# Moving the two kinds of transposes of an attention into the first gap of each step

## The chip, the cores and the metric

The kernel runs on one core of a Trainium2 chip. The metric is the time of one execution on the device in microseconds. The profile shows five engines: TensorE (PE; its weight loads are listed apart as PEld), VectorE (DVE), ScalarE (ACT), GpSimd (POOL) and SyncE (SP), which here only issues transfers. All data is 32-bit floating point.

## The reference

Eight batch items of 1024 tokens with 256 features pass through two layers. Each layer normalizes its input and adds the outputs of an attention and of a feed-forward part to it:

```python
xn = layernorm(x)
x = x + causal_attention(xn) + top1_experts(xn)      # 16 heads of 16, 8 experts, softmax router
xn = layernorm(x)
x = x + metric_attention(xn) + butterfly_ffn(xn)     # 16 heads of 16, 256 -> 1024 -> 256
```

In the first attention a query may see the keys up to itself (masked scores are a large negative number and not left out, so a small term for the masked keys stays in numerator and denominator). The second attention has no mask; its queries are multiplied by a metric computed from the input. In both, with one head's queries, keys and values:

```python
prob = softmax(q @ k.T / 4)
out  = prob @ v
```

The change concerns this attention. The experts and the butterfly part matter only as other work that TensorE does in between.

## The kernel before

**Units.** There are 16 attentions: the causal one (tiles named `_a`) and the unmasked one (`_b`) of each of the eight items, in an order that interleaves the two layers of neighbouring items. An attention has four groups `g` of four heads, and a group has two halves `h` of 512 queries. A half runs over tiles of 128 keys, `kt`: eight in the unmasked attention, four or eight in the causal one. One such (`g`, `h`, `kt`) is a *step*. A step has two parts `pr`, each for two of the group's four heads. I call the room for other work after the scores of part 0 the *first gap* and after those of part 1 the *second gap*.

**Scores and their maxima.** `exp_step` (its matmuls are L478) computes transposed scores of two heads, each with 32 rows of the array, into a pair of PSUM banks `sc`; ScalarE takes the exponential into `p` (L485), and in the causal attention GpSimd sets masked elements to zero (L487). The maximum of each query has to be known by then. So a first pass runs ahead: `max_step` computes scores with queries on the partitions into a pair of banks `mx` (L435), and VectorE reduces them to `mm` (L444). In the loop, `first_pass(1 - pr ...)` follows `exp_step(pr)`, so that the two use different rows of the array and run at once.

**Turn of the maxima.** When a half's maxima are complete, `maxima` writes their negatives to `negmax`, queries on the partitions. `put_max` (L464) turns them into the layout of Q^T with four 128x128 transposes into a pair bank `nm` (L468), and VectorE adds them to Q^T in a row that was kept free (L470). The local function `put(until)` (L1333) calls it for halves that became ready before half-step `until`; at the beginning of a half whatever is needed is put in any case.

**Weighing, and turn of the weighed values.** `weigh` (L500, matmuls L503) multiplies the exponentials with the values of four heads, each head 32 columns of the array, and sums over `kt` in the bank `av`. It runs one step late: in the first gap of a step it takes the `pair` of the step before, kept in `held`. When it has taken the last `kt` of a half, ScalarE copies `av` to `u` (L514), and the inner function returns what `norm` needs, which is kept in `turned`. `norm` (L517) turns `u` with four transposes into a pair bank `ut` (L523). In the unmasked attention VectorE then takes the reciprocal of the denominators (L550) and multiplies (L551). In the causal one GpSimd first prepares the terms for masked keys, `es` (L537) and `ec` (L542), and VectorE adds them (L546, L548) before the same two operations. The result goes to `on`, which the output projection reads later through `outputs`.

**Order and buffers.** The program order is written by hand. Pair banks come from a ring of three (`ps_sc`), used in turn by `sc`, `mx`, `nm`, `ut` and some of the other work; `av` has one bank, and other work has one (`ps_ms`). The projections of the next group of heads (`project0`, `project1`: tiles `q`, `k`) are called in both gaps of some steps as `urgent`; all else (experts, butterflies, normalization, output projections) is given out by `Fill`, which spends estimated costs against due times, mostly in the second gap. Neither kind of turn has a cost in these estimates, so where turns stand does not influence what `Fill` gives out.

## Time and profile before

| | |
|---|---|
| median of three runs | 4849.75 us (4848.44 to 4857.87) |
| the profiled execution's own time | 4851.03 us |
| its span, first to last instruction | 4849.3 us |
| mean granted TensorE clock | 0.988 |
| TensorE busy | 4665.7 us |
| VectorE, ScalarE, GpSimd busy | 3090.5, 2215.8, 765.0 us |
| scores and maxima's scores, `sc_b`, `mx_b` (L478, L435) | 1141.2, 1154.2 us, overlapping |
| weighing, `av_b`, `av_a` (L503) | 554.1, 338.9 us |
| turn of weighed values, `ut_a`, `ut_b` (L523) | 42.2, 41.8 us, 64 of four transposes each |
| turn of maxima, `nm_a`, `nm_b` (L468) | 44.9, 42.0 us, 64 of four transposes each |

Columns of a time line are start and duration in us, engine, line, operation, output<-inputs, shape and count; a bracket at the end gives how long the engine had been idle and what released it. In this profile a matmul of two 32-bit operands has two records and a transpose one, so a turn is x4 and the weighing of one part's two heads x4 as well; the time line merges neighbours. Busy times of one group are unions in time; groups that run in different rows of the array overlap.

### The profile page before, as it was taken

Reading aid. Unit: us, or ns where it says so; the run is one execution under the profiler, and the core shown is the slowest. Engines: PE = TensorE matmul, PEld = TensorE weight load, DVE = VectorE, ACT = ScalarE, POOL = GpSimd, SP = SyncE. Lnnn points to the kernel's source line nnn. Section 1 sums busy time; section 2 is a strip of 40 time slices with the busy share of each in tenths; the row PEclk is TensorE's granted clock in tenths of the full one; section 3 lists DMA queues with packets and bytes.
Section 4 is the critical chain, followed back from the end, with each engine's and each line's share of the span. In section 5 each row is a group of like instructions: output and inputs, shape, how many; then the busy total and the mean of one; then the engine's idle time right before and its main releaser. Section 6 shows DMA issues by size and latency. Waiting matters only on the chain.

```text
span 4849.3 us, 69199 instructions
## 1 busy us (share of the span) xinstructions
PE 4665.7 (96%) x27808; PEld 1865.1 (38%) x27808; DVE 3090.5 (64%) x5048; ACT 2215.8 (46%) x2925; POOL 765.0 (16%) x1340
## 2 busy tenths in 40 slices
PE   6899999999999999999999999999999999999998
PEld 3343344344333443334433444334443344433332
DVE  6776665665766567665676656766567665666553
ACT  2443444543454344543445434454345543454544
POOL 4232202111021110211112021111111111110000
PEclk8999999999999999999999999999999999999999
DMA  4122101120001200011000110001100110000000
GB/s 162 59 67 66 34 1 32 34 74 14 1 18 39 73 15 1 24 41 67 14 2 29 51 52 13 7 28 53 46 12 9 32 53 32 20 1 10 1 10 9
DMA packets 85680, 158.28 MB, mean 33 GB/s; under 512 B 12656, under 2 KB 67568, under 8 KB 82160
## 3 DMA queue, kind: packets, MB, share of 16 engines
q1 hardware_dynamic: 69616, 89.88, 5.5%
q0 software_dynamic: 15744, 63.98, 4.3%
q8 instruction: 220, 3.60, 0.3%
q14 instruction: 100, 0.82, 0.1%
HBM read 117.25 MB, written 36.57 MB: 32 GB/s over the span
## 4 chain that ended last, share of the span: by engine, by line
PE 88%; DVE 7%; ACT 3%; DMA 1%; issue 1%; POOL 0%; POOLq 0%; DVEq 0%; SPq 0%; ACTq 0%
PE sc_b L478 18%; PE av_b L503 10%; PE sc_a L478 10%; PE mx_b L435 6%; PE av_a L503 6%; PE w L1164 5%; PE mx_a L435 5%; PE f L390 5%; PE g_b L1091 3%; PE h_b L390 2%; PE e L811 2%; DVE mm_a L444 2%; ACT p_b L485 1%; PE q_a L390 1%; PE k_a L390 1%; PE q_b L390 1%
## 5 line engine op out<-in xcount | busy, mean ns | idle before, releaser
L444 DVE TENSOR_REDUCE mm_b<-mx_b 128x2 f32<-128x1024 f32 x1024 | 1251.5, 1223 | 756.6 <-PE mx_b L435 755.8
L485 ACT ACTIVATE p_b<-sc_b 128x1024 f32<-128x1024 f32 x1024 | 1044.8, 1023 | 1105.3 <-PE mx_b L435 619.1
L435 PE MATMUL mx_b<-kT_b,qT_b 32*128 32x512 f32 x4096 | 1154.2, 640 | 10.6 <-ACT p_b L485 6.8
L478 PE MATMUL sc_b<-qT_b,kT_b 32*128 32x512 f32 x4096 | 1141.2, 638 | 8.7 <-ACT p_b L485 2.6
L485 ACT ACTIVATE p_a<-sc_a 128x1024 f32<-128x1024 f32 (+3 forms) x768 | 620.1, 809 | 916.8 <-PE sc_a L478 640.4
L444 DVE TENSOR_REDUCE mm_a<-mx_a 128x2 f32<-128x1024 f32 (+3 forms) x768 | 733.9, 957 | 218.3 <-PE mx_a L435 199.2
L478 PE MATMUL sc_a<-qT_a,kT_a 32*128 32x512 f32 (+3 forms) x3072 | 713.3, 542 | 9.0 <-DVE mm_a L444 6.9
L435 PE MATMUL mx_a<-kT_a,qT_a 32*128 32x512 f32 (+3 forms) x3072 | 707.2, 542 | 10.2 <-ACT p_a L485 4.9
L503 PE MATMUL av_b<-p_b,vals 128*32 128x512 f32 x4096 | 554.1, 605 | 1.5 <-ACT p_b L485 1.5
L478 PEld LDWEIGHTS sc_b<-qT_b,kT_b 32*128 32x128 f32 x4096 | 305.9, 183 | 625.9 <-issue 418.3
L440 DVE TENSOR_TENSOR mx_a<-mx_a,cst 128x256 f32<-128x256 f32 x512 | 219.8, 429 | 342.0 <-PE mx_a L435 153.3
L487 POOL TENSOR_SCALAR_AFFINE_SELECT p_a<-p_a 128x256 f32<-128x256 f32 x512 | 210.0, 412 | 1410.0 <-ACT p_a L485 1380.1
L478 PEld LDWEIGHTS sc_a<-qT_a,kT_a 32*128 32x128 f32 x3072 | 235.6, 186 | 384.2 <-issue 269.8
L503 PE MATMUL av_a<-p_a,vals 128*32 128x512 f32 (+3 forms) x3072 | 338.9, 505 | 0.8 <-POOL spacer_a L707 0.7
L435 PEld LDWEIGHTS mx_b<-kT_b,qT_b 32*128 32x128 f32 x4096 | 306.3, 183 | 54.5 <-ACT p_b L485 39.9
L1164 PE MATMUL w<-wcon,f 128*128 128x256 f32 x1024 | 273.7, 396 | 0.0
L796 POOL DMA_INDIRECT ew<-in_ew,rows_a x120 | 116.5, 971 | 959.3 <-PE mx_b L435 443.0
L435 PEld LDWEIGHTS mx_a<-kT_a,qT_a 32*128 32x128 f32 x3072 | 233.9, 186 | 57.5 <-ACT p_a L485 33.9
L503 PEld LDWEIGHTS av_b<-p_b,vals 128*32 128x32 f32 x4096 | 81.7, 108 | 392.2 <-issue 383.2
L1164 PEld LDWEIGHTS w<-wcon,f 128*128 128x128 f32 x1024 | 178.2, 189 | 139.3 <-issue 114.5
L390 PE MATMUL f<-xT_b,wexp 128*128 128x512 f32 x512 | 223.9, 595 | 0.0
L503 PEld LDWEIGHTS av_a<-p_a,vals 128*32 128x32 f32 x3072 | 62.6, 108 | 265.4 <-issue 207.2
(215 smaller groups left out, 4232.4 us busy)
## 6 DMA issues: line engine op xcount, KB each, us to landing
ew<-sorted_d SPq DMA_DIRECT2D x120, 128.0 KB, 3.1
mixed_d<-ew SPq DMA_DIRECT2D x120, 128.0 KB, 1.7
x<-in_x SPq DMA_DIRECT2D x8, 1024.0 KB, 5.5
wexp<-wexp_d SPq DMA_DIRECT2D x8, 1024.0 KB, 7.6
wcon<-wcon_d SPq DMA_DIRECT2D x8, 1024.0 KB, 4.9
out<-x SPq DMA_DIRECT2D x8, 1024.0 KB, 5.0
paths<-in_paths SPq DMA_DIRECT2D x7, 1024.0 KB, 13.4
w<-in_w1t SPq DMA_DIRECT2D x8, 512.0 KB, 3.9
```

Source lines behind the costliest of these rows:

```text
L390: PE.matmul(ps, w[:, c, cols : cols + P], rhs[:, c, h * 512 : (h + 1) * 512], start=(c == 0), stop=(c == 1),)
L435: PE.matmul(sc[:, j, :w], qT[r : r + 32, t * P : (t + 1) * P], kT[r : r + 32, k * 512 : k * 512 + w], start=True, stop=True,)
L440: DVE.tensor_tensor(sc[:, :, w - P : w], sc[:, :, w - P : w], negmask.unsqueeze(1).to_broadcast([P, 2, P]), ALU.add,)
L444: DVE.tensor_reduce(mm[:, t, 2 * pr : 2 * pr + 2, k], sc[:, :, :w], AX.X, ALU.max)
L478: PE.matmul(sc[:, j, c0:], kT[r : r + 32, kt * P : (kt + 1) * P], qT[r : r + 32, h * 512 + c0 : (h + 1) * 512], start=True, stop=True,)
L485: ACT.activation(p[:, :, c0:], sc[:, :, c0:], AF.Exp, scale=0.25)
L487: POOL.affine_select(p[:, :, c0 : c0 + P], p[:, :, c0 : c0 + P], [[0, 2], [1, P]], ALU.is_ge, 0.0, base=0, channel_multiplier=-1,)
L503: PE.matmul(av[32 * i : 32 * i + 32, c0:], self.vals[:, kt, 4 * (g // 2) + i, odd : odd + 2, :].rearrange("p e d -> p (e d)"), p2[i // 2][ ...
L796: POOL.indirect_dma_start(halves[:, s % 2, : 3 * D], None, a["ew"], bass.IndirectOffsetOnAxis(ap=rows[:, s : s + 1], axis=0),)
L811: PE.matmul(ps[:, :D], was[:, c * P : (c + 1) * P], w[:, c * D : (c + 1) * D], start=(c == 0), stop=(c == 1),)
L1091: PE.matmul(ps, w2t[:, m, c * P : (c + 1) * P], hT[:, m, :], start=(m == 0), stop=(m == 3),)
L1164: PE.matmul(ps[:, :D], hT[k // 4][:, k % 4, i * P : (i + 1) * P], wcon[:, k, :], start=(k == 0), stop=(k == 7),)
```

## The change

In the first gap, the loop now calls `norm` for a finished half if one waits in `turned`, then the weighing of `held`, then `put`. In the second gap it calls none of the three. Before, the first gap had the weighing and then `put`; the second gap had `norm` and then `put`. A half that finishes its weighing in the first gap of a step was turned in the second gap of the same step; it is now turned in the first gap of the next step. The calls after the loop and the mandatory `put` at the start of a half are as they were.

```diff
                     for j in range(quota()):
                         first_pass(1 - pr if j == 0 else pr)
-                    if pr == 0 and held is not None:
-                        turned = weigh(*held)
-                    elif turned is not None:
-                        turned[0].norm(*turned[1:])
-                        turned = None
-                    put(now - 1)
+                    if pr == 0:
+                        if turned is not None:
+                            turned[0].norm(*turned[1:])
+                            turned = None
+                        if held is not None:
+                            turned = weigh(*held)
+                        put(now - 1)
                     if urgent is not None:
```

## The prediction

> **What bounds the kernel now.** I read the page first (busy time, then the chain that ended last), then the groups of instructions by shape, and then the time line of TensorE alone around two places where the moved work stands now. From the page: TensorE is busy for 96% of the span, and 88% of the chain lies on it; VectorE is busy for 64% and ScalarE for 46%. So the question is what each move does to the sequence on TensorE, and which short waits lie in it.

> ```profile
> PE 4665.7 (96%) x27808; PEld 1865.1 (38%) x27808; DVE 3090.5 (64%) x5048; ACT 2215.8 (46%) x2925; POOL 765.0 (16%) x1340
> ...
> PE 88%; DVE 7%; ACT 3%; DMA 1%; issue 1%; POOL 0%; POOLq 0%; DVEq 0%; SPq 0%; ACTq 0%
> ```

> The time line of TensorE shows three steps in the second attention, at 3054.18, 3059.14 and 3063.79. Columns: start, duration, engine, line, operation, tiles. I read starts, not durations, because the ends are modelled. `av` is the weighing, `nm` the turn of the maxima, `ut` the turn of the weighed values, `y` a piece of other work, `sc` and `mx` the scores (second rounds left out).

> ```profile
> 3054.18 1.06 PE L503 MATMUL av_b<-p_b,vals 128*32 128x512 f32 x8
> 3055.18 0.66 PE L468 MATMUL nm_b<-cst,negmax 128*128 128x128 f32 x4
> 3055.77 0.70 PE L478 MATMUL sc_b<-qT_b,kT_b 32*128 32x512 f32 x2
> ...
> 3056.84 1.13 PE L867 MATMUL y_a<-outw,oT_a 128*128 128x256 f32 x4
> 3057.90 0.70 PE L478 MATMUL sc_b<-qT_b,kT_b 32*128 32x512 f32 x2
> 3058.08 0.70 PE L435 MATMUL mx_b<-kT_b,qT_b 32*128 32x512 f32 x2
> ...
> 3059.14 1.06 PE L503 MATMUL av_b<-p_b,vals 128*32 128x512 f32 x8
> 3060.13 0.70 PE L478 MATMUL sc_b<-qT_b,kT_b 32*128 32x512 f32 x2
> ...
> 3061.27 0.66 PE L523 MATMUL ut_b<-cst,u_b 128*128 128x128 f32 x4
> 3061.76 1.03 PE L867 MATMUL y_a<-outw,oT_a 128*128 128x256 f32 x4
> 3062.72 0.70 PE L478 MATMUL sc_b<-qT_b,kT_b 32*128 32x512 f32 x2
> ...
> 3063.79 1.06 PE L503 MATMUL av_b<-p_b,vals 128*32 128x512 f32 x8
> 3064.78 0.70 PE L478 MATMUL sc_b<-qT_b,kT_b 32*128 32x512 f32 x2
> 3065.03 0.70 PE L435 MATMUL mx_b<-kT_b,qT_b 32*128 32x512 f32 x2
> ...
> 3066.09 1.13 PE L867 MATMUL y_a<-outw,oT_a 128*128 128x256 f32 x4
> ...
> 3068.22 0.64 PE L503 MATMUL av_b<-p_b,vals 128*32 128x512 f32 x4
> ```

> Four readings. A weighing alone takes 0.99 (3059.14 to 3060.13). A turn behind the weighing takes 0.59 more (3055.18 to 3055.77). A turn ahead of a piece of other work takes only 0.39 more: `ut` and `y` together 1.45 (3061.27 to 3062.72), `y` alone 1.06 (3056.84 to 3057.90). And there is a short wait: at 3064.78 `sc` starts and `mx` beside it only at 3065.03, so that this round of scores lasts 1.31 instead of 1.07. On ScalarE's time line the exponential of the scores before runs from 3063.95 to 3064.97; it holds the PSUM buffer that `mx` is to get. In the step with the turn of the maxima that wait (0.24) is filled, but 0.18 of it comes back after `y` (3057.90 to 3058.08). The steps last 4.96, 4.65 and 4.43.

> The second place is a step that computes the next projection, where `q` stands behind the weighing and `k` in the second gap:

> ```profile
> 3096.34 1.06 PE L503 MATMUL av_b<-p_b,vals 128*32 128x512 f32 x8
> ...
> 3100.32 0.66 PE L523 MATMUL ut_b<-cst,u_b 128*128 128x128 f32 x4
> 3100.82 1.98 PE L390 MATMUL k_b<-vT_b,wqk 128*128 128x512 f32 x4
> ...
> 3103.81 1.07 PE L503 MATMUL av_b<-p_b,vals 128*32 128x512 f32 x8
> ...
> 3108.29 1.98 PE L390 MATMUL k_b<-vT_b,wqk 128*128 128x512 f32 x4 [0.43 <-DVE qT_b L1116]
> ...
> 3111.27 0.64 PE L503 MATMUL av_b<-p_b,vals 128*32 128x512 f32 x4
> ```

> The step with the turn lasts 7.47, the one without 7.46: the turn sits in time in which `k` would wait for VectorE to empty the single small PSUM bank (0.43 in the second step). Here the turn is free today.

> **The change part by part.** I compared the instruction order of both kernels, engine by engine. Without the lines of `norm`, all five engines have the same order in both. So the turn of the maxima, `put_max`, moves nowhere: it stood in a first gap already (124 of its 128 directly behind a weighing). That part costs and gains nothing, and neither DMA nor ScalarE nor SyncE issues anything in another order. What moves is `norm`: 127 of its 128 turns go from the second gap of a step to the first gap of the next, ahead of the weighing. No instruction is added or removed.

> On TensorE, 118 of the 127 stood ahead of other work with the same 128x128 shape, 9 stood alone between scores. Going through the trace step by step, 31 turns are in a projection step followed by another one, 84 have an ordinary piece behind them and one in the next step, and 12 lack one of the two.

> The price in the new place is not in the trace: a weighing always follows scores there. Two rows are near: 0.59 for a turn and a weighing in one gap in the other order, 0.39 for a turn whose neighbour has its own shape. I take 0.59, because the neighbour is the weighing and its shape (128x32) differs from the turn's; 0.39 stays as the lower end. It cannot be below that where no wait is next to it, as TensorE does the same four products.

> [...]

> Projection steps: the second gap saves nothing (7.47 against 7.46, the wait for `q` takes the turn's place), the first gap has no wait to fill (scores behind `q` take 1.07). 31 x 0.59 = +18.3; lower end 31 x 0.39 = 12.1.

> Ordinary steps: the second gap saves 0.39. The first gap costs 0.59, fills the wait of 0.24, and 0.18 returns after the piece behind it; that is the step at 3054.18 against the one at 3063.79, 4.96 - 4.43 = 0.53. 0.53 - 0.39 = 0.14. Without the 0.18 (a long piece behind, which covers the exponential) it is -0.04; where the trace has no wait behind the weighing (28 of the 84) it is 0.20; with the saving read from whole steps (4.65 - 4.43 = 0.22) it is 0.31. I take 0.13, near the first and a little under it for the long pieces: 84 x 0.13 = +10.9, ends 84 x (-0.04) = -3 and 84 x 0.31 = +26.

> The other 12: alone between scores, where the exponential sets the pace, a turn is partly hidden today; between -0.4 (its 0.59 really saved, the wait filled at the new place) and +0.59. I take 0.1: +1.2.

> VectorE and GpSimd: per turn VectorE has 0.67 (0.25 + 0.42) in the second attention and 1.25 (0.41, 0.17, 0.25, 0.42) in the first; they move behind the reduction of the next scores (1.22). Nothing on TensorE needs the result before the output projection, several steps on. What waits is the PSUM buffer, reused one round later; the turn of the maxima, with 0.69 on VectorE in the same gap, shows scores at 1.07 behind it, so I cost this at 0. On GpSimd, `es` and `ec` (0.62 and 0.22) of 41 causal turns go behind masks (25, 0.41 each) and gathers (18, about 0.97): VectorE waits longer for `es`, now 17 us in 19 waits. It idles 0.9 before the next reduction, which hides most of that; if not, see the third rival.

> Sum: 18.3 + 10.9 + 1.2 = +30.4. The profiled execution took 4851.0 (span 4849.3 and 1.7 around it), 1.3 above the median of the runs. 4851.0 + 30.4 - 1.3 = 4880.

> **The rivals.** Against no change I count 0.2%, 9.7 us, about what a measurement of this kernel can tell.

> 1. No price for going from the turn to the weighing: each of the three groups falls by 0.20 a turn. 31 x 0.39 + 84 x (-0.07) + 12 x (-0.1) = 12.1 - 5.9 - 1.2 = +5: 4855, no measurable change. For it: turn to `y` is free. Against: weighing to turn is not.

> 2. Faster: VectorE is what holds the scores up. Today `norm`'s 0.67 or 1.25 stand right behind a reduction in the second gap; moved, all that VectorE gives back in that gap comes earlier. Over the affected pairs of steps, the rounds of scores next to the old and the new place last 39 us over 1.07 each, and the projections' waits come to 17.4: 56 in all. The gross price without any wait filled is 127 turns x 0.59 less 84 x 0.39, or 42; the change is faster once over 42 of the 56 vanish, and all 56 gone would make 4850 - 14 = 4836. Against: most of these waits end with ScalarE's exponential, and VectorE sat idle for 1.63 before it took `q`.

> 3. Slower than forecast: the 41 causal turns whose `es` queues behind GpSimd's masks and gathers hold VectorE, and with it the PSUM buffers. At 0.6 each, +25: 4905.

> **How the numbers follow.** Forecast 0.71, first rival 0.12, second 0.08, third 0.09. The predicted time is 4880. The range 4854 to 4900 takes in the first rival and the upper end of the sum (18.3 + 26 + 7 = 51, nearly), and leaves out the second and third. Slower 0.80 (forecast and third), same 0.12, faster 0.08.

> **What would show it.** In the profile after: `ut` starts, then `av` about 0.59 later (0.39 if the first rival holds); scores behind such a gap at 1.07, and `mx` 0.18 late after the next piece; projection steps with the turn near 8.05, those that lost it still near 7.46 with a wait for `qT`. I am wrong if `av` follows `ut` at 0.4, if the waits for VectorE in projection steps go away, or if scores behind the new place wait for `mm`.

## The result, and the profile after

| | before | after |
|---|---|---|
| median of four runs each | 4852.57 us (4848.44 to 4857.87) | 4884.23 us (4881.49 to 4888.69) |
| the profiled execution's own time | 4851.03 us | 4884.23 us |
| its span | 4849.3 us | 4882.5 us |
| mean granted TensorE clock in it | 0.988 | 0.985 |

The changed kernel takes 1.007 times as long (95% interval 1.0057 to 1.0082), 31.7 us more. The page of the changed kernel, busy time and chain:

```profile
PE 4687.2 (96%) x27808; PEld 1864.1 (38%) x27808; DVE 3099.1 (63%) x5048; ACT 2214.6 (45%) x2925; POOL 764.0 (16%) x1340
...
PE 87%; DVE 7%; ACT 3%; DMA 1%; issue 1%; POOL 1%; SPq 0%; POOLq 0%; DVEq 0%; ACTq 0%
```

The counts of instructions are the same as before, TensorE has 21.5 us more and is still busy for 96%. So nothing new bounds the kernel; its own sequence got longer. The time line of TensorE in the changed kernel, for the two steps that answer to those at 3059.14 and 3063.79 before (columns: start, duration, engine, line, operation, tiles):

```profile
3082.27 1.06 PE L503 MATMUL av_b<-p_b,vals 128*32 128x512 f32 x8
3083.27 0.70 PE L478 MATMUL sc_b<-qT_b,kT_b 32*128 32x512 f32 x2
...
3084.40 1.13 PE L867 MATMUL y_a<-outw,oT_a 128*128 128x256 f32 x4
3085.46 0.70 PE L478 MATMUL sc_b<-qT_b,kT_b 32*128 32x512 f32 x2
3085.58 0.70 PE L435 MATMUL mx_b<-kT_b,qT_b 32*128 32x512 f32 x2
...
3086.64 0.66 PE L523 MATMUL ut_b<-cst,u_b 128*128 128x128 f32 x4
3087.22 1.06 PE L503 MATMUL av_b<-p_b,vals 128*32 128x512 f32 x8
3088.22 0.70 PE L478 MATMUL sc_b<-qT_b,kT_b 32*128 32x512 f32 x2
3088.23 0.70 PE L435 MATMUL mx_b<-kT_b,qT_b 32*128 32x512 f32 x2
...
3089.29 1.13 PE L867 MATMUL y_a<-outw,oT_a 128*128 128x256 f32 x4
3090.35 0.70 PE L478 MATMUL sc_b<-qT_b,kT_b 32*128 32x512 f32 x2
3090.53 0.70 PE L435 MATMUL mx_b<-kT_b,qT_b 32*128 32x512 f32 x2
...
3091.59 0.64 PE L503 MATMUL av_b<-p_b,vals 128*32 128x512 f32 x4
```

From `ut` to `av` it is 0.58 (3086.64 to 3087.22). The scores behind the gap last 1.07 (3088.22 to 3089.29), and `mx` is 0.18 late behind the piece `y` (3090.35 to 3090.53). The step that lost the turn lasts 4.37 instead of 4.65: it saves 0.29 and not 0.39, because there too `mx` is now a little late behind `y` (0.12, 3085.46 to 3085.58). The step that got it lasts 4.95 instead of 4.43.

The second place, two steps with a projection, same view of the changed kernel:

```profile
3119.54 1.06 PE L503 MATMUL av_b<-p_b,vals 128*32 128x512 f32 x8
3120.53 1.98 PE L390 MATMUL q_b<-vT_b,wqk 128*128 128x512 f32 x4
...
3124.02 1.98 PE L390 MATMUL k_b<-vT_b,wqk 128*128 128x512 f32 x4 [0.43 <-DVE qT_b L1116]
...
3127.01 0.65 PE L523 MATMUL ut_b<-cst,u_b 128*128 128x128 f32 x4
3127.59 1.06 PE L503 MATMUL av_b<-p_b,vals 128*32 128x512 f32 x8
3128.59 1.98 PE L390 MATMUL q_b<-vT_b,wqk 128*128 128x512 f32 x4
...
3132.08 1.98 PE L390 MATMUL k_b<-vT_b,wqk 128*128 128x512 f32 x4 [0.43 <-DVE qT_b L1116]
...
3135.06 0.64 PE L503 MATMUL av_b<-p_b,vals 128*32 128x512 f32 x4
```

The first step has lost the turn and still lasts 7.47: the wait of 0.43 for VectorE stands where the turn was. The second has gained it and lasts 8.05, with the same wait.

Both kernels have 896 steps in the same order, so that I could subtract them one by one (a step runs from the start of one weighing, or of the turn ahead of it, to the next). In the 31 pairs of projection steps the first step changed by -0.3 in all and the second by +18.3. In the 84 ordinary pairs the steps that lost the turn changed by -32.5, those that got it by +45.4 and the two behind by -2.7, together +10.2. The other 12 places give -10.0, +6.4 and +5.6 a step later, +2.0. That is 30.2 of the 31.8 by which the steps of the two profiles differ; 1.4 more lies ahead of the first step and makes the 33.2 between the spans.

### The profile page after: what moved, and what is told of

It is laid out like the page before. It is cut to its first block, busy times and chain, and to the rows that moved or that the text cites. A ratio compares the mean times of both kernels' runs of the same rounds, so it can differ in the third digit from the quotient of the medians.

```text
span 4882.5 us, 69095 instructions
## 1 busy us (share of the span) xinstructions
PE 4687.2 (96%) x27808; PEld 1864.1 (38%) x27808; DVE 3099.1 (63%) x5048; ACT 2214.6 (45%) x2925; POOL 764.0 (16%) x1340
## 4 chain that ended last, share of the span: by engine, by line
PE 87%; DVE 7%; ACT 3%; DMA 1%; issue 1%; POOL 1%; SPq 0%; POOLq 0%; DVEq 0%; ACTq 0%
PE sc_b L478 18%; PE av_b L503 10%; PE sc_a L478 10%; PE mx_b L435 6%; PE av_a L503 6%; PE w L1164 5%; PE mx_a L435 5%; PE f L390 5%; PE g_b L1091 3%; PE h_b L390 3%; PE e L811 2%; DVE mm_a L444 1%; PE k_b L390 1%; PE q_b L390 1%; PE y_a L867 1%; PE k_a L390 1%
## 5 line engine op out<-in xcount | busy, mean ns | idle before, releaser
L435 PE MATMUL mx_b<-kT_b,qT_b 32*128 32x512 f32 x4096 | 1157.7, 641 | 11.4 <-ACT p_b L485 7.7
L478 PE MATMUL sc_b<-qT_b,kT_b 32*128 32x512 f32 x4096 | 1139.3, 638 | 6.9 <-DVE mm_b L444 1.9
L478 PE MATMUL sc_a<-qT_a,kT_a 32*128 32x512 f32 (+3 forms) x3072 | 717.0, 544 | 7.9 <-DVE mm_a L444 6.4
L435 PE MATMUL mx_a<-kT_a,qT_a 32*128 32x512 f32 (+3 forms) x3072 | 709.5, 544 | 11.4 <-DVE mm_a L444 5.9
L503 PE MATMUL av_b<-p_b,vals 128*32 128x512 f32 x4096 | 554.7, 605 | 1.5 <-ACT p_b L485 1.5
L478 PEld LDWEIGHTS sc_b<-qT_b,kT_b 32*128 32x128 f32 x4096 | 305.8, 183 | 624.4 <-issue 433.1
L478 PEld LDWEIGHTS sc_a<-qT_a,kT_a 32*128 32x128 f32 x3072 | 237.7, 188 | 386.7 <-issue 258.1
L503 PE MATMUL av_a<-p_a,vals 128*32 128x512 f32 (+3 forms) x3072 | 339.9, 507 | 0.8 <-POOL spacer_a L707 0.7
L435 PEld LDWEIGHTS mx_b<-kT_b,qT_b 32*128 32x128 f32 x4096 | 306.9, 183 | 55.9 <-ACT p_b L485 42.8
L435 PEld LDWEIGHTS mx_a<-kT_a,qT_a 32*128 32x128 f32 x3072 | 235.5, 188 | 58.8 <-ACT p_a L485 37.3
L390 PE MATMUL f<-xT_b,wexp 128*128 128x512 f32 x512 | 223.9, 595 | 0.0
L503 PEld LDWEIGHTS av_b<-p_b,vals 128*32 128x32 f32 x4096 | 81.9, 108 | 355.6 <-issue 346.1
L503 PEld LDWEIGHTS av_a<-p_a,vals 128*32 128x32 f32 x3072 | 62.7, 109 | 232.1 <-issue 170.1
```

The lines of the kernel that those rows point to most:

```text
L390: PE.matmul(ps, w[:, c, cols : cols + P], rhs[:, c, h * 512 : (h + 1) * 512], start=(c == 0), stop=(c == 1),)
L435: PE.matmul(sc[:, j, :w], qT[r : r + 32, t * P : (t + 1) * P], kT[r : r + 32, k * 512 : k * 512 + w], start=True, stop=True,)
L478: PE.matmul(sc[:, j, c0:], kT[r : r + 32, kt * P : (kt + 1) * P], qT[r : r + 32, h * 512 + c0 : (h + 1) * 512], start=True, stop=True,)
L503: PE.matmul(av[32 * i : 32 * i + 32, c0:], self.vals[:, kt, 4 * (g // 2) + i, odd : odd + 2, :].rearrange("p e d -> p (e d)"), p2[i // 2][ ...
```

## The experiments

The kernel before was measured again beside each group of experiments: its median was 4853.4 us beside experiments 1 to 4, 4853.9 beside 5 to 8, 4857.4 beside 9 to 11 and 4849.7 beside 12. Each kernel is compared with the runs taken beside it.

**1. The shapes by themselves.** A kernel with nothing but TensorE's four kinds of work, each cycle 24 times in a row (`REPS`), with no other engine at work: N is a turn, W a weighing of both parts, F a product of 128x256, S the scores of two pair banks.

```diff
+CYCLES = ("N", "W", "F", "S", "NW", "NF", "WF", "SW", "SN", "SF", "SNW", "SWN", "SNF", "SFW", "SWF")
...
+    do = {"N": turn, "W": weighing, "F": full, "S": scores}
+    for cycle in CYCLES:
+        for _ in range(REPS):
+            for c in cycle:
+                do[c]()
```

> This kernel leaves the whole computation out. TensorE runs short cycles of the four kinds of matmuls of the real kernel, each cycle 24 times, with nothing to wait for: N a turn (four 128x128 transposes), W a weighing (eight matmuls into 32 columns each), F a piece of other work (two matmuls 128x128 by 256), S scores (four matmuls of 32 rows each). Theory of the shapes: a turn costs about 0.44 in a row of turns; from the first transpose to the first matmul of a weighing behind it 0.55 to 0.60, as in the changed kernel (0.586), and to a piece F behind it 0.44 to 0.50, although no engine but TensorE works. Rival, that a wait for another engine or a PSUM buffer made the 0.59: with nothing to wait for, turn to weighing takes the same 0.44 to 0.50 as turn to F.

The time line of TensorE in this kernel, a stretch of the cycle scores, turn, weighing, and one of the cycle scores, turn, product:

```profile
452.48 0.66 PE L36 MATMUL ut<-ident,x 128*128 128x128 f32 x4
453.06 1.92 PE L41 MATMUL av<-x 128*32 128x512 f32 x16
454.92 0.70 PE L58 MATMUL sc<-x 32*128 32x512 f32 x2
...
455.99 0.66 PE L36 MATMUL ut<-ident,x 128*128 128x128 f32 x4
...
613.12 0.66 PE L36 MATMUL ut<-ident,x 128*128 128x128 f32 x4
613.62 1.03 PE L49 MATMUL ot<-x 128*128 128x256 f32 x4
614.58 0.70 PE L58 MATMUL sc<-x 32*128 32x512 f32 x2
```

Behind the turn the weighing starts after 0.58, the product of the turn's own shape after 0.50. By whole cycles: scores and weighing take 2.925, with a turn 3.511, so a turn beside a weighing costs 0.586, in either order. Scores and product take 2.132, with a turn 2.526, so there it costs 0.394. Alone, turn after turn takes 0.437 each, and a turn ahead of a product 0.436, so going on to other work of the same shape is free; a turn ahead of a weighing takes 0.585 and one ahead of scores 0.586. The 0.19 between 0.586 and 0.394 is therefore a price of TensorE alone; what TensorE does in that time no run shows. The first rival has no ground left.

**2. The other order in the same gap.** The changed kernel, with the turn behind the weighing.

```diff
                     if pr == 0:
-                        if turned is not None:
-                            turned[0].norm(*turned[1:])
-                            turned = None
+                        ready, turned = turned, None
                         if held is not None:
                             turned = weigh(*held)
+                        if ready is not None:
+                            ready[0].norm(*ready[1:])
                         put(now - 1)
```

> The changed kernel with the turn of the weighed values behind the weighing instead of ahead of it, in the same first gap. Theory of the shapes: weighing to turn changes the shape as turn to weighing does, so nothing changes in 93 of the 127 places; in the 34 where a projection or other 128x128 work follows in that gap, the turn now stands beside its own shape and costs 0.39 instead of 0.59: 34 x 0.2 = 7 us less than the changed kernel, so about 25 us over the kernel before. Rival, that VectorE's share of the turn in that gap makes the loss: its place is the same or later, so no less than the changed kernel, 32 over before.

4873.99 against 4853.38, ratio 1.0043 (1.0029 to 1.0056): 20.6 more, where 25 was expected. The median ordinary step did not change against the other order (weighing and turn 1.58 in both). In projection steps the turn now stands ahead of `q`, which has its own shape, and the second steps gained 12.9 in place of 18.3 (median 0.419 each). So the price follows the neighbour's shape here too. In the profiles 5.4 us of the difference to the changed kernel is this; 5.2 more is one step near 355 us that had a wait of 3.40 for VectorE and then half the clock in the changed kernel alone.

**3 and 4. The two parts apart.** In the changed kernel, some turns go back to the second gap: in experiment 3 the 31 of the projection steps, so that the other 96 alone are moved; in experiment 4 the 96, so that the 31 alone are moved. The lines are those of 3; in 4 the condition is `urgent is None`.

```diff
+                    elif urgent is not None and turned is not None:
+                        turned[0].norm(*turned[1:])
+                        turned = None
```

> The 31 turns that stood ahead of k in a projection step go back to the second gap; the other 96 are moved as in the change. Theory of the shapes: the 31 were 18.3 of the sum, so about 12 us over the kernel before (10.9 + 1.2), 19 to 20 under the changed one. Rival, that each moved turn costs alike by what it does on VectorE: 96/127 of 32 us, 24 over before.

> Only the 31 turns ahead of k in a projection step are moved to the first gap of the next step; the other 96 stay where they were. Theory of the shapes: 31 x 0.59 = 18 us over the kernel before, all of it between the start of ut and the start of av in the second projection step, which then lasts about 8.05, while the first stays at 7.47 with a wait for qT. Rival, that each moved turn costs alike: 31/127 of 32 us, 8 over before.

The 96 outside projection steps alone: 4866.7, ratio 1.0029 (1.0019 to 1.0039), 13.3 more, where 12 was expected. Projection steps alone: 4884.66, ratio 1.0063 (1.0049 to 1.0077), 31 more, where 18 was expected. The sum of the parts, 44, is more than the whole, 32, so something else was in these times. Step by step, in experiment 4, the projection pairs had their 18.3 (0.587 each) and the ordinary steps about 0. The other 12 lay in the start of the kernel (+5.4 in the first 62 steps) and behind it in steps in which the granted clock was halved for a while (+6.6). The steps that ran at full clock both here and in the kernel before (some 863 of 895) do add up: they are 4.6 longer in experiment 3, 19.6 in experiment 4 and 22.7 in the changed kernel. So a good part of the 13.3 of experiment 3 belongs to the clock too. Experiments 9 to 12 go after the clock.

**5. GpSimd's part early.** In the changed kernel, `es` and `ec` of a causal half are issued in the second gap, as before the change, and only the turn and VectorE's part go into the first gap (`mask_terms` issues the two, and `norm` takes their results from `masked`).

```diff
+        def mask_terms(self, g, h):
...
+                if (g, h) not in self.masked:
+                    self.mask_terms(g, h)
+                es, ec = self.masked.pop((g, h))
...
+                    elif turned is not None and turned[0].causal:
+                        turned[0].mask_terms(*turned[1:3])
```

> The changed kernel, but GpSimd's two operations of a causal turn (es, ec) are issued where they were before the change, in the second gap of the step before; only the transposes and VectorE's part stand in the first gap. Theory of the shapes: nothing on TensorE's path changes, so the changed kernel within 4 us, some 28 to 36 over the kernel before. Third rival of the prediction (GpSimd's queue holds VectorE and with it PSUM buffers): at least 5 us less than the changed kernel, up to 25.

4888.84, ratio 1.0074 (1.0061 to 1.0087): 35 more than before, and no gain over the changed kernel. The steps have the same length as in the changed kernel (median difference 0.00). GpSimd's queue costs nothing here, and the third rival falls.

**6. VectorE's part longer.** In the changed kernel the last multiplication of each turn is issued twice.

```diff
             DVE.tensor_tensor(
                 mine_of(self.on[h]), num, rc.unsqueeze(3).to_broadcast([P, 4, 4, 16]), ALU.mult
             )
+            DVE.tensor_tensor(
+                mine_of(self.on[h]), num, rc.unsqueeze(3).to_broadcast([P, 4, 4, 16]), ALU.mult
+            )
```

> The changed kernel with VectorE's last operation of each turn (0.42, L551) done twice: 128 x 0.42 = 54 us more work on VectorE in the first gap. Theory of the shapes: VectorE is not what the first gap waits for; within 8 us of the changed kernel. Second rival of the prediction (VectorE's queue decides what a turn costs): about 0.42 for most of the 128 turns, 30 to 54 us over the changed kernel.

4893.21, ratio 1.0085 (1.0072 to 1.0099): 39 more than before, some 8 more than the changed kernel (39.3 against 31.7). In ordinary steps the difference is 0.00; some second steps of projections got 0.29 longer, 4.9 in all. So 128 further instructions on VectorE are nearly covered. Had VectorE's part held the scores up in the first gap, it would have been 30 or more. The second rival, which forecast a faster kernel, falls with the result itself, and its premise with this experiment.

**7. The turns where they are free.** The kernel before, with 32 turns (first halves of even groups) held back until the second gap of the projection's second step.

```diff
-            u = work.tile([P, 512], F32, tag="u", name=f"u_{self.n}_{g}_{h}", bufs=1)
+            u = work.tile([P, 512], F32, tag="u", name=f"u_{self.n}_{g}_{h}", bufs=2)
...
                     if pr == 0 and held is not None:
                         turned = weigh(*held)
-                    elif turned is not None:
-                        turned[0].norm(*turned[1:])
-                        turned = None
+                        if turned is not None and turned[1] % 2 == 0 and turned[2] == 0:
+                            late, turned = turned, None
+                    elif pr == 1:
+                        if turned is not None:
+                            turned[0].norm(*turned[1:])
+                            turned = None
+                        elif late is not None and i % 2 and h == 0 and kt == 1:
+                            late[0].norm(*late[1:])
+                            late = None
```

> The kernel before, with one turn in four moved elsewhere: the turn of the first half of groups 0 and 2 is kept (two buffers for u instead of one) until the second gap of the second projection step, ahead of k, where TensorE waits 0.43 for VectorE today. Theory (a turn is free where it fills a wait beside its own shape): 32 turns cost nothing there beyond about 0.06 each and save 0.22 to 0.39 at their old place: 5 to 10 us under the kernel before. Rival, that the second projection step has no such wait once VectorE has the turn's 0.67 to 1.25 there as well: no gain, or some us over the kernel before.

The time line of TensorE in this kernel, in the second of two projection steps:

```profile
3100.84 1.06 PE L503 MATMUL av_b<-p_b,vals 128*32 128x512 f32 x8
3101.83 1.98 PE L390 MATMUL q_b<-vT_b,wqk 128*128 128x512 f32 x4
...
3104.82 0.66 PE L523 MATMUL ut_b<-cst,u_b 128*128 128x128 f32 x4
3105.32 1.98 PE L390 MATMUL k_b<-vT_b,wqk 128*128 128x512 f32 x4
```

The turn stands in the place of the wait for `q`, and the step still lasts 7.47. The places that lost a turn got 14.5 shorter in all, the places that got one 0.2 longer. Yet the median is 4853.35 against 4853.9, ratio 0.9998 (0.9989 to 1.0007): the gain of 5 to 10 worked out is not in the time. In the profile, behind the first 62 steps, all steps at full clock together are 13.9 shorter, and the steps with a halved clock 13.0 longer.

**8. Both turns in the second gap.** The opposite of the change: `put` goes there as well.

```diff
-                    if pr == 0 and held is not None:
-                        turned = weigh(*held)
-                    elif turned is not None:
-                        turned[0].norm(*turned[1:])
-                        turned = None
-                    put(now - 1)
+                    if pr == 0:
+                        if held is not None:
+                            turned = weigh(*held)
+                    else:
+                        if turned is not None:
+                            turned[0].norm(*turned[1:])
+                            turned = None
+                        put(now - 1)
```

> The kernel before, with the turns of the maxima moved the other way: put is called in the second gap alone, so that 121 of these turns stand ahead of other work of their own shape (none beside the weighing). If only shapes count: 121 x 0.2 = 24 us less, about 4829. What I expect: VectorE adds the turned maxima to Q^T behind the reduction of the scores before (1.22), and the first scores of the next half read Q^T; the second gap is some 1.45 long, the sum is there 2.1 after its start, so these scores wait about 0.65: 121 x 0.65 = 79 less the 24, some 50 us over the kernel before.

4908.55, ratio 1.0106 (1.0091 to 1.012): 55 more. TensorE's time line in this kernel shows why the turn of the maxima is no match for a place ahead of a piece of its own shape:

```profile
3091.67 0.66 PE L468 MATMUL nm_b<-cst,negmax 128*128 128x128 f32 x4
3092.16 1.03 PE L867 MATMUL y_a<-outw,oT_a 128*128 128x256 f32 x4
3093.76 0.70 PE L478 MATMUL sc_b<-qT_b,kT_b 32*128 32x512 f32 x2 [0.56 <-DVE qT_b L470]
```

`y` follows at the cheap 0.49, but the next scores wait 0.56 for VectorE to add the maxima to Q^T. The waits of TensorE in this kernel (total, times, longest) have 51.5 us of this kind, where the kernel before has 1.2:

```profile
PE sc_b L478 <- DVE qT_b L470: 35.2, 48, 1.5
PE sc_a L478 <- DVE qT_a L470: 16.3, 16, 2.3
```

The 126 steps with such a turn got a median of 0.30 longer, 29.4 in all: about these 51.5 less the 24 that the cheaper neighbour was to save. That is about half of the 55. The mean granted clock of this profile is 0.979 against 0.988, and of the 58 by which all its steps are longer 37.5 lie in steps that met a halved clock in one of the two kernels (some of the 29.4 among them). So the expectation of 50 had the wait right and was met in its size with the clock's help. For the turn of the maxima the first gap is right, for the turn of the weighed values the second.

**9 to 12. The halved clock taken away where it can be.** TensorE waits 4.0 to 4.2 us for a fetch of the experts in each of the later five items. The waits of TensorE in the kernel before (the costliest; total, times, longest):

```profile
PE e L819 <- DMA ew<-sorted_d: 29.7, 11, 4.2
```

One of them on the time line of the kernel before, and the same place in its table by windows (busy time of each engine, then PEclk, the granted clock, then the DMA share and GB/s):

```profile
2238.55 1.13 PE L811 MATMUL e<-ew,et 128*128 128x256 f32 x4 [0.52 <-DVE et L822]
2243.88 0.69 PE L819 MATMUL e<-cst,ew 128*128 128x128 f32 x2 [4.20 <-DMA ew<-sorted_d]
2245.09 2.08 PE L811 MATMUL e<-ew,et 128*128 128x256 f32 x4 [0.52 <-DVE et L822]
```

```profile
2236.00:2242.00 6.00, 3.16 (x15) 2.21 (x13) 1.60 (x4) 0.00 (x0) 1.01 (x1) 1.00 0.16 39
2242.00:2248.00 6.00, 3.60 (x18) 2.15 (x22) 1.18 (x4) 0.00 (x0) 0.00 (x0) 0.50 0.25 93
```

Behind the wait the same product takes 2.08 in place of 1.13, and the clock is 0.50. The experiment puts products that nobody reads into the wait, in four kernels: the one before, 7, 4 and the changed one.

```diff
+            if s == NS - 1 and b >= 3:
+                for _ in range(7):
+                    PE.matmul(ps[:, D:], ident, was, start=True, stop=True)
             if s < NS:
                 was = work.tile([P, D], F32, tag="gT", name=f"et_{b}_{s}")
```

> The kernel before, with seven 128x256 products of the identity and an expert's tile put in front of the last transposes of the experts' tokens of five items, into the half of the bank that the transposes overwrite: work that nobody reads, about 3.6 us, in the place of a wait of 4.0 to 4.2 us for the fetch. If the halved clock after this wait comes from TensorE standing idle, the five stretches of 6.8 to 13.7 us at 0.5 near 1648, 2242, 2832, 3423 and 4013 us go away; of each some 4.9 us hold work, which loses half of it, so 5 x 2.4 = 12 us less than the kernel before, about 4841. If the low clock has another cause, or the filler merely delays the transposes, the time stays at 4853 or rises by up to 5 x 0.5.

> The same filler in the kernel that turns 32 halves in the second gap of the projection's second step. Undisturbed steps were 13.9 us shorter there, and the time the same because more stretches of low clock came up. If these follow short waits of about 1 us (0.31 and 0.70 for VectorE near 1795, 2386, 2980, 3570) and not the wait for the fetch, the filler takes the five long ones away here as well and the others stay: about 4841, as the kernel before with the filler. If all came from the wait for the fetch, 4841 - 14 = 4827.

> The same filler in the kernel that moves the turns of the projection steps alone. It was 31 us slower than the kernel before where 18.3 was worked out. If the 11 to 13 too many come from the clock after the wait for the fetch, it is 18 slower than the kernel before with the filler, about 4860; if from elsewhere, still 31 slower, about 4872.

> The filler in the changed kernel. The kernel before with the filler took 10.7 us less than the kernel before. If the 31 us of the change come from its own steps alone, as the sum of 30.4 said, this kernel is 30 slower than that one: about 20 slower than the kernel before. If some 10 us of the 31 come from the halved clock after the wait for the fetch (undisturbed steps of the changed kernel's profile add up to 21.5), it is about 10 slower than the kernel before.

| kernel | without filler | with filler | the kernel before, beside it | ratio of the last two |
|---|---|---|---|---|
| before | 4852.57 | 4846.64 | 4857.35 | 0.998 (0.9968 to 0.9991) |
| 7, turns into projections | 4853.35 | 4834.91 | 4857.35 | 0.9953 (0.994 to 0.9966) |
| 4, projections alone | 4884.66 | 4862.15 | 4857.35 | 1.0011 (1.0002 to 1.0019) |
| changed | 4884.23 | 4865.79 | 4849.69 | 1.0036 (1.0022 to 1.0049) |

The time line of the kernel before with the filler, at the same place:

```profile
2237.77 3.19 PE L817 MATMUL e<-et,cst 128*128 128x256 f32 x14
2242.20 0.44 PE L822 MATMUL e<-cst,ew 128*128 128x128 f32 x2 [1.25 <-DMA ew<-sorted_d]
2243.16 1.73 PE L811 MATMUL e<-ew,et 128*128 128x256 f32 x4 [0.52 <-DVE et L825]
```

The filler lasts 3.2, not the 3.6 that I had worked out, and 1.25 of waiting is left. In this item one shorter stretch at half clock stayed behind the fetch (1.73 for the product); in the other four items none. Two stretches came up elsewhere, near 1800 and 3568. What the four runs show:

- The kernel before gained 10.7 (4857.35 to 4846.64; the interval leaves about 4 to 16) by work that nobody needs. The stretches behind the fetch cost about what was worked out (12).
- With the filler, the projection steps alone cost 15.5 (4862.15 against 4846.64, measured side by side), near the 18.3 of the step-by-step sum, and not 31 (the two intervals together leave about 8 to 22). So most of the 12 too many of experiment 4 goes with the halved clock.
- With the filler, experiment 7's gain is there: 11.7 (4846.64 to 4834.91; the intervals leave about 3 to 20), 22.4 below the kernel before. The 4834.91 lies between the two expectations, 4827 and 4841: short stretches near 1791, 2378, 2969 and 3556 stayed. This kernel is the fastest of all.
- The changed kernel with the filler is 1.0036 / 0.998 = 1.0056 times the kernel before with it, 27 us; the half-widths of both intervals, added in squares, leave about 18 to 36. That lies between the two expectations (30 and 20 over the kernel before with the filler). So the change's own steps carry most of the 31.7; these runs alone can't tell the few us between 27 and 31.7 from nothing.

## Why the prediction was right, step by step

**What moves.** Right: the `norm` turns alone moved. The turn of the maxima has the same neighbours and the same time as before (step at 3077.32 after: 4.95, at 3054.18 before: 4.96).

**The price in the new place.** Taken as 0.59 from the other order, with 0.39 as the lower end. Over 127 places the median from `ut` to `av` is 0.586 (0.558 to 0.589). Experiment 1 shows that the order doesn't matter and that no other engine has a part in it. In its cycles of turns and weighings alone, going from a turn to a weighing takes 0.15 more than going on to another turn (0.585 against 0.437), and going back 0.14 more than going on to another weighing (1.855 against 1.717). The runs show this price, not what TensorE does in that time.

**Projection steps, +18.3.** Measured +18.3 in the steps that got the turn and -0.3 in those that lost it. The wait for `q` did take the turn's place.

**Ordinary steps, +10.9.** Measured +10.2, or 0.12 a pair for the 0.13 taken. The pair shown above costs 0.23, since its old place saved 0.29 only; over all 84 the median saving is 0.391 and the median cost 0.544. Steps at half clock are in the +10.2; the 80 places that met none, in the pair and the two steps behind, come to 0.08 each, which would be 6.6 for 84.

**The other 12, +1.2.** Measured +2.0, but this is no confirmation: it is -10.0 and +6.4 in the two steps and a single +5.6 a step later. That step took 10.07 for 4.42: it had a wait of 3.40 for VectorE and 5.4 us at half clock, where before it had neither. Without it the 12 places are -3.6.

**VectorE and GpSimd at 0.** Experiments 5 and 6 agree: GpSimd's part issued early gained nothing, and 54 us more on VectorE cost some 8.

**The sum.** 30.4 forecast, 31.8 over the steps of the two profiles, 31.7 between the medians (4884.2 for the 4880 forecast). What the sum did not have is the granted clock, and experiments 4 and 7 missed their expectations by 13 and by 5 to 10 largely for want of it. Of the 31.8, the 863 steps that ran at full clock in both profiles hold 22.7, of which 18.1 are the projection steps; the 32 steps that met a halved clock in one of the two hold 9.1. Up to TensorE's last instruction the changed kernel has 139.9 us at half clock, the kernel before 109.2. So the direction, the mechanism and the largest term were right, the ordinary steps and the other 12 together came out some 7 too high, and the steps that met a halved clock, which had no term, made up for it. That the sum met the median within 1.3 us is luck to that extent.

**The rivals.** No price for going from turn to weighing: excluded by the 0.586. VectorE holding the scores up: excluded by the sign of the result and by experiment 6. GpSimd's queue: excluded by experiment 5.

## What to carry to other kernels

A short piece of work on the engine that bounds this kernel was priced by its neighbours: four transposes cost 0.39 beside work of their own shape, 0.59 beside another, and nothing measurable inside a wait (7.47 with the turn, 7.46 without). Before moving such a piece, look for the wait that it fills now, since that is lost with it. And before a difference of some ten us is explained by the order of instructions, compare the granted clock of the two executions, and subtract the traces step by step: the steps that the edit touches tell its price even where the total hides it.

## What the runs showed of the hardware

**Two short waits in one grid step did it too.** In places two waits of 0.31 and 0.70 us were followed by half the clock. TensorE's time line in experiment 7, and the granted clock there by windows:

```profile
2383.89 0.66 PE L468 MATMUL nm_a<-cst,negmax 128*128 128x128 f32 x4 [0.31 <-DVE mm_b L444]
2384.47 0.49 PE L478 MATMUL sc_a<-qT_a,kT_a 32*128 32x128 f32 x4
2385.66 1.83 PE L435 MATMUL mx_b<-kT_b,qT_b 32*128 32x512 f32 x4 [0.70 <-DVE mm_b L444]
```

```profile
2379.20:2386.00 6.80, 5.79 (x46) 2.70 (x40) 6.50 (x14) 2.06 (x6) 2.88 (x6) 1.00 0.06 19
2386.00:2396.20 10.20, 10.20 (x38) 4.32 (x35) 4.04 (x5) 2.52 (x3) 1.69 (x3) 0.50 0.05 14
```

1.01 us of waiting, and then 10.2 us at half the clock. This came back in four items in a row (near 1795, 2386, 2980 and 3570). The kernel before has the same two waits in its five later items (0.34 and 0.70), and no stretch of half clock behind any of them. What differs is where they fall on the grid. Laid on the grid of each profile, the two waits stand together in one grid step 17 times in the 12 profiles that have them, and all 17 times a stretch begins with the next grid step. They reach over two grid steps 43 times, and a stretch follows 4 times; all five pairs of the kernel before are of this kind. But a wait of 1.45 ahead of a turn of the maxima (in the kernel before near 1691, 2282 and so on) lies within one grid step 54 times over all 13 profiles and was never followed by half the clock. So the time waited in a grid step does not decide alone, and what else does stays open.

**The spread of the runs goes with it.** In the 11 runs of experiment 7 the time follows the mean granted clock: 4842 to 4846 at 0.987, 4849 to 4854 at 0.985, 4858 at 0.983, 4864 at 0.982. One thousandth of the clock is 4 to 5 us.
